# V's seven block products with 128 moving columns a matmul in place of 256, in a two-layer graph attention kernel

## The chip, the cores and the metric

The kernel runs on one core of one Trainium2 chip. The metric is the device time of one execution in microseconds (us). Three runs of the kernel before are given; the median is 2369.56 us.

## The reference

There are 128 graphs of 128 nodes with 512 features each (`x`: 128 x 128 x 512, fp32) and one 128 x 128 adjacency matrix for each graph. Two layers follow one another, each with a residual and a layer norm:

```python
def layer0(x, adj):                          # multi-head attention, 8 heads of 64
    q, k, v = x @ Wq + bq, x @ Wk + bk, x @ Wv + bv
    logits = einsum('bqhd,bkhd->bhqk', q, k) / sqrt(64)
    attn = softmax(where(adj > 0, logits, -1e9), axis=-1)
    return relu(einsum('bhqk,bkhd->bqhd', attn, v) @ Wo + bo)

def layer1(h, adj):                          # one-head graph attention
    Wh = h @ W
    e = leaky((Wh @ a1)[:, :, None] + (Wh @ a2)[:, None, :])
    att = softmax(where(adj > 0, e, -9e15), axis=1)
    return leaky(einsum('bij,bjf->bif', att, Wh))

x = layernorm(x + layer0(x, adj))
x = layernorm(x + layer1(x, adj))
```

The change touches only `x @ Wv`, the product that makes V.

## The kernel before

**Tiling.** Graphs are worked on in groups of four (`GROUP = 4`), that is 512 tokens; there are 32 groups. For each group, `products(g)` makes Q, K and V. Each of the three is a 512 x 512 by 512 x 512 product in fp32, done by Strassen's scheme on 256 x 256 blocks: seven block products in place of eight, with sums of blocks formed beforehand and results added afterwards. `group_product` holds it: `multiply` issues the TensorE work of one block product, `read` copies a partial sum out of PSUM on ScalarE (ACT), `add` adds a PSUM block to such a copy on VectorE (DVE) and writes a quarter of the result.

**One block product.** A block product contracts over 256 (two steps `kc` of 128) and gives 256 x 256 (two halves `m` of 128 rows). So `multiply` issues four calls of `nc.tensor.matmul`, each with a stationary block of 128 x 128 and a moving block of 128 x 256. In the profile every fp32 call appears as two pairs of records, LDWEIGHTS (engine PEld, the load of the stationary block) and MATMUL (engine PE), so a block product is 8 loads and 8 matmuls, and the seven of a group are 56 of each.

**Which operand is stationary.** For Q and K (`transposed_out=True`) the weight block is stationary and x moves, so the result has features on the partitions. For V (`transposed_out=False`) the block of x (128 tokens) is stationary and the weight block moves: 256 columns of features. V's weight blocks don't stay on chip. `wv` is in DRAM, and `fetch` brings one block product's weights at a time into a ring of three tiles:

```python
        def fetch():
            if todo:
                n = todo.pop(0)
                ring[n] = work.tile([P, 2, HALF], F32, name="wv_n", bufs=3)
                nc.sync.dma_start(ring[n], wv[n])
```

In the trace V's instructions are therefore those of line L367 that read `wv_n`; Q's and K's read `wq` and `wk` at the same line. The PSUM tiles are `st_y`, `st_w` and `st_x`, one bank each, 128 x (2 x 256) fp32.

**Other TensorE work.** `pair_product` (L448) does the same scheme for pairs of graphs with `wo` and `w1`, at 256 or 257 moving columns. `Softmax.scores` (L520, tile `lg`) multiplies 64-row operands with 128 moving columns, in the two row halves of the array alternately. `Softmax.attend` (L600, tile `p_oT`) uses 64-column stationary blocks with 128 moving columns, in the two column halves alternately. `Edge.product` (L841, tile `p_h`) has 512 moving columns. A few transposes (`p_x`, `p_e`, `p_busy`) load a 128 x 128 block and move 128 columns.

**Order.** The kernel writes the order of all instructions on every engine by hand (`manual_schedule` for TensorE, VectorE, ScalarE, SyncE and GpSimd). A loop over graphs calls `group()` and `pair()` between the steps of the softmax and the edge attention, so that block products stand between the pieces of other work; the last four graphs follow a written plan. [...]

Of the kernel before, what the change touches and what calls it, by code (L numbers as in the profile page):

```python
# [24 lines left out]
def kernel(  # L25
# [59 lines left out]
    nc = tc.nc  # L85
    B, P, D = x.shape
# [208 lines left out]
    def strassen(bank, multiply, read, add):  # L295

        p, t = {}, {}

        def product(role, n, start=False):
            def run():
                if start:
                    p[role] = bank(role)
                multiply(p[role], n, start)

            return run

        def copy(name, o):
            def run():  # L310
                t[name] = read(name, p["y"], o)

            return run

        def block(h, o, role, name=None):
            return lambda: add(h, o, p[role], t.get(name))

        return {
            "p1": product("y", 0, True),
            "t0": copy("t0", 0),  # L320
            "p5": product("w", 4, True),
            "p6": product("y", 5),
            "t2": copy("t2", 1),
            "p2": product("x", 1, True),
            "c11": block(0, 0, "x", "t0"),
            "p7": product("y", 6),
            "t3": copy("t3", 1),
            "c22": block(1, 1, "w", "t3"),
            "p4": product("y", 3),
            "c21": block(1, 0, "y"),  # L330
            "p3": product("w", 2),
            "c12": block(0, 1, "w", "t2"),
        }
# [7 lines left out]
    def copy_out(dst, p, o, bias):  # L341

        if bias is None:
            nc.scalar.copy(dst, p)  # L344
            return
        for m in range(2):
            col = bias[:, 2 * o + m : 2 * o + m + 1]
            nc.scalar.activation(dst[:, m, :], p[:, m, :], AF.Identity, bias=col)  # L348

    def group_product(g, turn, weight, out, transposed_out, bias=None):  # L350

        def bank(role):

            tag = "abc"[("ywx".index(role) - turn) % 3]
            return ps_st.tile([P, 2, 2 * P], F32, name=f"st_{role}", tag=tag)

        def multiply(p, n, start):
            w, xs = weight(n), XS[g][n]  # L360
            for m in range(2):
                cols = slice(m * P, (m + 1) * P)
                for kc in range(2):
                    lhs, rhs = xs[:, kc, cols], w[:, kc, :]
                    if transposed_out:
                        lhs, rhs = w[:, kc, cols], xs[:, kc, :]
                    nc.tensor.matmul(  # L367
                        p[:, m, :],
                        lhs,
                        rhs,  # L370
                        start=start and m == 0 and kc == 0,
                        stop=True,
                        skip_group_check=True,
                    )

        def read(name, p, o):
            t = work.tile([P, 2, 2 * P], F32, name=f"st_{name}")
            copy_out(t, p, o, bias)
            return t

        def add(h, o, p, t):
            if t is None:
                copy_out(out(h, o), p, o, bias)
            else:
                nc.vector.tensor_add(out(h, o), p, t)

        return strassen(bank, multiply, read, add)

    def products(g):
# [1033 lines left out]
```

## Time and profile before

| What | Value |
|---|---|
| Median of 3 runs | 2369.56 us (2368.99 to 2372.61) |
| Profiled execution | span 2364.5 us from its first to its last instruction |
| Device time less span | 5.1 us, with the median of the runs (the page gives no own time for the profiled execution beside its span) |
| TensorE clock granted, mean | 0.998 |
| PE busy, matmul records | 2330.4 us, 13362 records |
| PEld busy, weight-load records | 1976.3 us, 13362 records |
| DVE, ACT, POOL busy | 1836.7, 1507.4, 769.9 us |
| Mean DMA rate | 167 GB/s |
| V's matmul records (line L367 on `wv_n`) | 1792, which is 32 groups of 56 |

How to read it: a record of PE is one matmul and its duration contains a pipeline that overlaps the next record. So the duration of a record (379 ns for 256 columns) is not the step from one record to the next (some 216 ns). Where a stream of matmuls is at stake, the step between starts counts. A load (PEld) is recorded for each matmul and lies beside the matmul in front of it.

### The profile page before, as it was taken

The page shows a single profiled execution, that of the slowest core. Times are in us where ns is not written, and L with a number is a line of the kernel's source. Part 1 is how long each engine was busy: PE and PEld are TensorE (multiplying, and loading weights), DVE is VectorE, ACT ScalarE, POOL GpSimd, SP SyncE. Part 2 cuts the span into 40 slices and gives each one's busy share as a digit, 9 for nine tenths or more (in the row PEclk, how much of TensorE's full clock was granted, in tenths as well). Part 3 has the DMA queues.
Part 4 walks back from the last instruction along what each step waited for, and adds up shares of the span by engine and source line. Part 5 has one row for each costly group of instructions (what it writes and reads, how often), then busy time and mean ns, then how long its engine had stood idle before and what let it go on. Part 6 is the DMA issues. An engine that isn't in the chain of part 4 may idle for free.

```text
span 2364.5 us, 43985 instructions
## 1 busy us (share of the span) xinstructions
PE 2330.4 (99%) x13362; PEld 1976.3 (84%) x13362; DVE 1836.7 (78%) x3718; ACT 1507.4 (64%) x5459; POOL 769.9 (33%) x1191
## 2 busy tenths in 40 slices
PE   8999999999999999999999999999999999999997
PEld 7878888888888888888888888888888888888875
DVE  5677787877878877878778778778787787787778
ACT  3656666667666666666576666666665766666675
POOL 2232333323333323333233333233332333332325
PEclk9999999999999999999999999999999999999999
DMA  6655555555555555555555555555555555555453
GB/s 196 189 158 164 169 165 178 163 164 169 173 158 175 166 168 165 168 170 173 163 171 167 163 175 168 168 163 170 172 169 164 170 168 163 176 167 168 152 164 114
DMA packets 435564, 395.31 MB, mean 167 GB/s; under 512 B 108280, under 2 KB 339328, under 8 KB 435328
## 3 DMA queue, kind: packets, MB, share of 16 engines
q1 hardware_dynamic: 435008, 392.23, 54.2%
q8 instruction: 107, 1.75, 0.3%
q14 instruction: 129, 1.06, 0.2%
q10 hardware_dynamic: 320, 0.26, 0.0%
HBM read 248.58 MB, written 143.72 MB: 166 GB/s over the span
## 4 chain that ended last, share of the span: by engine, by line
PE 85%; DVE 5%; DMA 4%; ACT 3%; issue 1%; SPq 1%; POOL 1%; DVEq 0%; POOLq 0%; ACTq 0%
PE st_y L367 25%; PE p_y L448 16%; PE st_w L367 13%; PE p_w L448 8%; PE st_x L367 6%; PE lg L520 5%; PE p_oT L600 4%; PE p_h L841 4%; PE p_x L448 4%; ACT pa L568 1%; DMA paz<-pa_dram 1%; DMA pa_dram<-pa 1%; DVE st L644 1%; DVE pa L534 1%; DVE nmax L543 0%
## 5 line engine op out<-in xcount | busy, mean ns | idle before, releaser
L650 POOL TENSOR_SCALAR ve<-mv 128x1 f32<-128x1 f32 x256 | 69.8, 273 | 1425.4 <-DVE mv L646 1420.0
L554 ACT ACTIVATE pa<-pa,nmax 128x128 f32<-128x128 f32 x1008 | 393.4, 394 | 5.6 <-DVE nmax L543 5.5
L568 ACT ACTIVATE pa<-pa,rs 128x128 f32<-128x128 f32 x1008 | 326.6, 391 | 28.5 <-DVE rs L564 28.5
L344 ACT COPY st_t<-st_y 128x512 f32<-128x512 f32 x192 | 111.0, 578 | 158.9 <-PE st_y L367 83.2
L459 ACT COPY pr_t<-p_y 128x257 f32<-128x257 f32 (+1 forms) x375 | 137.3, 366 | 110.8 <-PE p_y L448 109.9
L348 ACT ACTIVATE st_t<-st_y,b_cols 128x256 f32<-128x256 f32 x192 | 79.9, 467 | 198.9 <-PE st_y L367 198.9
L554 ACT ACTIVATION_READ_ACCUMULATOR pa<-pa,nmax 128x1 f32 x1008 | 192.3, 191 | 0.0
L587 DVE STREAM_TRANSPOSE pa<-paz 128x1024 f32<-128x1024 f32 x126 | 156.9, 1245 | 18.1 <-DMA paz<-pa_dram 15.6
L534 DVE TENSOR_TENSOR pa<-lg,mf 128x512 f32<-128x512 f32 x252 | 161.0, 680 | 0.2 <-PE lg L520 0.2
L614 ACT ACTIVATE oT<-p_oT,b_cols 128x128 f32<-128x128 f32 x504 | 137.1, 381 | 33.8 <-PE p_oT L600 33.6
L543 DVE TENSOR_REDUCE nmax<-pa 128x8 f32<-128x1024 f32 x126 | 151.7, 1204 | 2.2
L652 POOL TENSOR_TENSOR rstd<-ve,mhalf 128x1 f32<-128x1 f32 x256 | 146.2, 571 | 21.3
L600 PEld LDWEIGHTS p_oT<-pa,v 128*64 128x64 f32 x2016 | 108.6, 137 | 49.5 <-issue 23.7
L520 PE MATMUL lg<-kT,qT 64*128 64x128 f32 x2048 | 132.1, 279 | 0.0
L448 PE MATMUL p_y<-wo,oT 128*128 128x256 f32 x504 | 129.6, 380 | 1.7 <-ACT p_y L469 1.7
L448 PE MATMUL p_y<-w,x1T 128*128 128x257 f32 x496 | 128.8, 382 | 1.7 <-ACT wk L459 1.6
L448 PE MATMUL p_y<-wo,oS 128*128 128x256 f32 x504 | 129.5, 379 | 0.5 <-ACT pr_t L459 0.5
L520 PEld LDWEIGHTS lg<-kT,qT 64*128 64x128 f32 x2048 | 119.4, 188 | 12.3 <-issue 11.6
L448 PE MATMUL p_y<-w,x1S 128*128 128x257 f32 x496 | 128.0, 380 | 0.2 <-ACT wk L459 0.2
L600 PE MATMUL p_oT<-pa,v 128*64 128x128 f32 x2016 | 125.0, 276 | 2.3 <-DVE pa L587 1.9
L367 PE MATMUL st_y<-wv_n,xT 128*128 128x256 f32 x512 | 121.3, 380 | 3.3 <-ACT st_t L344 3.3
L367 PE MATMUL st_y<-xT,wk 128*128 128x256 f32 x512 | 124.0, 385 | 0.0
(201 smaller groups left out, 5869.6 us busy)
## 6 DMA issues: line engine op xcount, KB each, us to landing
pa_dram<-pa SPq DMA_DIRECT2D x126, 512.0 KB, 2.9
paz<-pa_dram SPq DMA_DIRECT2D x504, 128.0 KB, 2.8
wv_n<-wv SPq DMA_DIRECT2D x224, 256.0 KB, 3.0
x<-in_x_dram SPq DMA_DIRECT2D x128, 256.0 KB, 2.9
x_dram<-x SPq DMA_DIRECT2D x128, 256.0 KB, 2.3
xz<-x_dram SPq DMA_DIRECT2D x512, 64.0 KB, 2.0
xz<-in_x_dram SPq DMA_DIRECT2D x496, 64.0 KB, 2.3
out_dram<-z SPq DMA_DIRECT2D x120, 256.0 KB, 2.5
```

The source lines that it names most:

```text
L367: nc.tensor.matmul(p[:, m, :], lhs, rhs, start=start and m == 0 and kc == 0, stop=True, skip_group_check=True,)
L448: nc.tensor.matmul(p[:, :width], xs()[n][:, kc, :], w[:, PLACE[n], kc, :], start=start and kc == 0, stop=True, skip_group_check=True,)
L459: nc.scalar.copy(t[:, :width], p[:, :width])
L520: nc.tensor.matmul(self.lg[r][:, c, :], q[rows, c, cols], k[rows, c, cols], start=c == 0, stop=True, skip_group_check=True,)
L534: nc.vector.tensor_add(by_head[:, r * NC : (r + 1) * NC], self.lg[r].rearrange("p c (b k) -> p c b k", b=4), mf.unsqueeze(1).to_broadcast( ...
L543: nc.vector.tensor_reduce(self.nmax, by_head, AX.XY, ALU.max, negate=True)
L554: nc.scalar.activation(self.pa[:, :, h, :], self.pa[:, :, h, :], AF.Exp, bias=self.nmax[:, h : h + 1], accum_out=self.sums[:, h : h + 1],)
L568: nc.scalar.activation(self.pa[:, :, h, :], self.pa[:, :, h, :], AF.Copy, scale=self.rs[:, h : h + 1])
L587: nc.vector.transpose(self.paT.rearrange("p h (a i) -> p a h i", i=32), self.paz.rearrange("p a (h k) -> p a h k", k=32),)
L600: nc.tensor.matmul(self.oT[r * HD : (r + 1) * HD, c, :], v[:, h * HD : (h + 1) * HD], self.paT[:, r * NC + c, :], start=c == 0, stop=True, ...
L614: nc.scalar.activation(OT[pair][:, c, h * P : (h + 1) * P], self.oT[:, c, :], AF.Identity, bias=b_cols[:, 1, c : c + 1],)
L652: nc.gpsimd.tensor_tensor(self.r, ve, mhalf, ALU.pow)
```

## The change

Where the output is not transposed, which holds for V alone, each call of 256 moving columns becomes two calls of 128 moving columns. The two calls use the same stationary block of x, and each call brings its own load of that block. The output columns, the order of the contraction steps and everything after the product stay. For Q and K `width` is 256 and the loop runs once. The `start` flag stays on the first call that writes into a fresh bank.

```diff
                     if transposed_out:
                         lhs, rhs = w[:, kc, cols], xs[:, kc, :]
-                    nc.tensor.matmul(
-                        p[:, m, :],
-                        lhs,
-                        rhs,
-                        start=start and m == 0 and kc == 0,
-                        stop=True,
-                        skip_group_check=True,
-                    )
+                    width = 2 * P if transposed_out else P
+                    for at in range(0, 2 * P, width):
+                        nc.tensor.matmul(
+                            p[:, m, at : at + width],
+                            lhs,
+                            rhs[:, at : at + width],
+                            start=start and m == 0 and kc == 0 and at == 0,
+                            stop=True,
+                            skip_group_check=True,
+                        )
```

A block product of V is then eight calls of 128 x 128 by 128 x 128 in the program's order, where it was four; the other engines' instructions and their order are those of before.

## The prediction

> **What bounds the kernel now.** I read the page's busy table first, then its slices, then the chain of work that ended last:
>
> ```profile
> span 2364.5 us, 43985 instructions
> PE 2330.4 (99%) x13362; PEld 1976.3 (84%) x13362; DVE 1836.7 (78%) x3718; ACT 1507.4 (64%) x5459; POOL 769.9 (33%) x1191
> PEclk9999999999999999999999999999999999999999
> PE 85%; DVE 5%; DMA 4%; ACT 3%; issue 1%; SPq 1%; POOL 1%; DVEq 0%; POOLq 0%; ACTq 0%
> ```
>
> PE is busy in every slice, at full granted clock, and 85% of the chain is PE. So TensorE's stream sets the time, and time added to that stream is added to the kernel unless it falls ahead of a stall that it fills. PE's busy time is made of records that overlap, so I don't count with it: I count steps from one matmul's start to the next. This is the timeline of PE early in the run, one row for a run of records (start, length, name, count):
>
> ```profile
> 10.37 1.04 PE L944 MATMUL p_x<-ident,x_turned 128*128 128x128 f32 x8
> 11.24 1.89 PE L367 MATMUL st_x<-xT,wq 128*128 128x256 f32 x8
> ...
> 20.83 1.89 PE L367 MATMUL st_y<-xT,wk 128*128 128x256 f32 x8
> 22.56 1.89 PE L367 MATMUL st_y<-xT,wq 128*128 128x256 f32 x8
> ```
>
> Eight records of 256 columns run from 20.83 to 22.56 us: 216 ns each. Eight transposes of 128 columns run from 10.37 to 11.24 us: 109 ns each. Taken from the individual starts in the trace, leaving stalls out: V's 256-column records step by 215.7 ns (1729 steps), transposes by 109.2 ns (17 steps).
>
> The next view is the groups by line with shapes kept apart (count, then busy us, mean ns, idle before):
>
> ```profile
> L520 PE MATMUL lg<-kT,qT 64*128 64x128 f32 x2048 | 132.1, 279 | 0.0
> L600 PE MATMUL p_oT<-pa,v 128*64 128x128 f32 x2016 | 125.0, 276 | 2.3 <-DVE pa L587 1.9 <-DVE rt L835 0.4
> L367 PE MATMUL st_y<-wv_n,xT 128*128 128x256 f32 x512 | 121.3, 380 | 3.3 <-ACT st_t L344 3.3
> L520 PEld LDWEIGHTS lg<-kT,qT 64*128 64x128 f32 x2048 | 119.4, 188 | 12.3 <-issue 11.6 <-DVE mf L498 0.3 <-DVE pa L534 0.3
> L600 PEld LDWEIGHTS p_oT<-pa,v 128*64 128x64 f32 x2016 | 108.6, 137 | 49.5 <-issue 23.7 <-PE st_y L367 22.0 <-DVE pa L587 2.6
> L367 PEld LDWEIGHTS st_y<-wv_n,xT 128*128 128x128 f32 x512 | 96.8, 190 | 18.0 <-ACT st_t L344 4.8
> ```
>
> A load's record depends on its columns: 137 ns for 64, 188 to 190 for 128, whether 64 or 128 rows take part. V's load (190 ns) today lies beside a matmul that takes 215.7 ns. The question is what such a load costs beside one of 109 ns.
>
> **What the Trainium skill says.** "TensorE: Matmul & The Clock Gate", section "LDWEIGHTS (loading the stationary operand)", puts a load at columns / 1.2 ns: 107 ns for 128, 53 for 64. The trace agrees in the slope (190 - 137 = 53 ns for 64 columns) and shows some 83 ns on top, which can be a latency that overlaps. The same page, "What happens when you issue a matmul", says that a load is pulled ahead of the matmul in flight into a background buffer; here each load starts 1 to 3 ns after the start of the matmul before it. Its "Back-to-back issue gap" gives N / 2.4 + 2.5 ns for a matmul alone, but 81 ns, not 56, for bf16 pairs of load and matmul at N = 128: that section warns of short moving blocks. "FP8 and Floating Point Precision", "TensorE Precision Notes", has true fp32 in four passes; each call here shows as two records, so two passes each: 2 x 256 / 2.4 + 2.5 = 215.8 ns against 215.7 measured, and 2 x 128 / 2.4 + 2.5 = 109.2 against 109.2.
>
> **The change, step by step.** Removed: 32 groups x 7 products x 8 = 1792 matmul records of 256 columns, with as many loads: 1792 x 215.7 ns = 386.5 us of TensorE's stream. Added: 3584 of 128 columns and 3584 loads of 128 x 128. Their step is the unknown.
>
> *Lower bound*, 109.2 ns: the array's own time, as in the transposes. Their loads have 141 ns records, so they don't test V's load. It gives 3584 x 109.2 - 386.5 = +4.9 us, which is one more fixed cost of some 2.5 ns for each old record.
>
> *The nearest rows.* L520 has loads of the full 128 columns (188 ns) beside 128 moving columns, and each row half of the array steps by 111.7 ns (1784 steps, 111 to 112); L600, with the short 137 ns loads, steps by 109.2. So a 188 ns load does not show its full record, only 107 ns and a handover of a few ns, and it is just longer than the matmul in front. L520 uses half the rows. The full array is seen where a transpose is followed by an ordinary matmul, whose 190 ns load must then hide behind 128 columns. A window of the groups view at such a place, ending within its first matmul:
>
> ```profile
> L944 PE MATMUL p_x<-ident,x_turned 128*128 128x128 f32 x3 | 0.5, 273 | 0.0
> L367 PE MATMUL st_x<-xT,wq 128*128 128x256 f32 x1 | 0.4, 382 | 0.0
> ```
>
> The matmul is recorded 109 ns after the transpose, but lasts 382 ns where its like last 379, and the next starts 219 ns on, not 216: it really began 3 ns late. Six of the transposes `p_e` near the end run into the next product without a stall: 108 to 110 ns, and where 257 or 256 columns follow (five), again 382 or 383 and 218 or 219. So 112 ns holds for the full array, once; sustained it is seen only in L520.
>
> *Value taken*: 111.7 ns. 3584 x 111.7 = 400.3 us, less 386.5: **+13.8 us**. By product: 16 x 111.7 - 8 x 215.7 = +61 ns on 1.73 us. *Upper bound*: if a full-array stream paid the 2.5 ns between 109.2 and 111.7 once more, 114.2 ns, +22.8 us.
>
> *The joints.* The record after a V product has its load behind 128 columns instead of 256, and the first record of a product still has a 256-column one in front of it; the count of short steps stays 3584. A semaphore that a next load waits for is needed no earlier than now: the last short matmul begins 109 ns later than the long one did. Before L520 and L600 the trace shows 309 ns after a 256-column record and 203 after a 128-column one: the same 94 ns, so nothing is lost there. The last record's tail shrinks from 379 to 272 ns but starts about 109 later: the readers on ACT and DVE get each product when its columns end, 61 ns later than now.
>
> *What hides some of it.* No wait, DMA or PSUM bank is added. The instruction stream grows by 3584 on PE; L520 runs two loads and two matmuls in 111.7 ns, twice V's density, so issue is not the limit: nothing. The weight fetches (`wv_n`, ring of three) have the same bytes, and start up to 61 ns later a product; covered by two ring tiles of lead. The `v` adds (DVE) and copies (ACT) wait for PE, and what stands behind them in order shifts with PE. A longer V fills stalls that other engines set. PE's waits:
>
> ```profile
> PE st_y L367 <- ACT st_t L344: 3.3, 3, 1.9
> PE st_y L367 <- DMA wv_n<-wv: 1.7, 1, 1.7
> PE st_w L367 <- DVE x1T L246: 0.5, 2, 0.3
> PE st_w L367 <- DMA wv_n<-wv: 0.3, 1, 0.3
> ```
>
> The ACT waits are in the first 200 us and follow from V's own copies. The rest, measured as starts later than the step allows, is three stalls behind DVE's x1T (832, 1050, 1267 us: 0.5, 0.4, 0.3) and four on `wv_n` (0.3 to 1.9 us, the largest at 2273): 4.4 us together. The fetches hang on PE's own release of the ring, so I credit little of those: 1.5 us absorbed in all (my choice; 0 to 4). **Sum: 13.8 - 1.5 = +12.3 us.** The sum stands against the profiled span, 2364.5 us, giving 2376.8; with the 5.1 us around it, which are the median less the span (the page has no time of its own for that execution), 2381.9, against the median of 2369.56: +0.52%.
>
> **The rivals.**
> *The load binds nowhere, so hardly anything shows* (not slower). The place is the handover from load to matmul: if the load of a full array in a stream is ready within the array's 109.2 ns, the bill is 4.9 us, less 1.5: +3.4 us, 2373.0. It decides below 109.5 ns, where the net falls under 4.7 us. Two runs differ by about 0.2% (4.7 us) before I would call them different. For: transposes and L600 step by 109.2. Against: their loads are short, and both places with full loads show 112. If the second load of the same block were left out, contrary to the change's words, this is the time as well. Below nothing I see no way: no column is saved and no wait is removed; the stalls it might move total 4.4 us.
> *Loads are not hidden in a stream.* The skill's 81 against 56 ns means 25 ns for each pair: 3584 x 25 + 4.9 = +94 us, about 2464. Wholly serial, 109 + 107 = 216 ns a record, would be +388 us. For: the section named, and that today's V never tests a load behind 109 ns. Against: L520 at 111.7, and the joints.
>
> **How the numbers follow.** The load just binds, 111 to 114.2 ns (2379 to 2392): 0.85, and this is the likeliest, 2381.9. Nothing binds: 0.09. Exposed loads, over 2400: 0.05. Something unforeseen that ends below -0.2%: 0.01. The range leaves out the exposed loads, and takes in the lower bound's case: 2373 to 2391. Chances: faster 0.01, within 0.2% 0.09, slower 0.90.
>
> **What would show it.** PE and PEld with 15154 records each. V's rows as 128x128, x3584, some 272 to 276 ns for a matmul and 188 to 192 for a load. A V product of 16 records in 1.79 us where eight took 1.73; Q's and K's still 1.73. Idle of PE unchanged within 3 us. Steps of 109 ns mean the first rival; steps over 120, or a V row with load idle in front, the second. I am also wrong if the steps are 112 but the time stays or grows otherwise: then stalls moved, and PE's waits must name them.

## The result, and the profile after

The changed kernel takes 2378.59 us (median of 4 runs, 2375.91 to 2381.42) against 2369.89 us for the kernel before (4 runs): +8.7 us, ratio 1.0041, 95% interval 1.0027 to 1.0054. The forecast was 2381.9 us, +12.3 us. A second measurement on another occasion gave 2375.32 us (18 runs) against 2367.28 us (28 runs): +8.0 us, ratio 1.0033, interval 1.0025 to 1.0042. So the kernel became slower by 0.3 to 0.4%.

The busy table, the granted clock and the chain of the page after, in the order in which those of before were shown:

```profile
span 2374.1 us, 47569 instructions
PE 2342.3 (99%) x15154; PEld 2040.3 (86%) x15154; DVE 1837.2 (77%) x3718; ACT 1511.9 (64%) x5459; POOL 770.5 (32%) x1191
PEclk9999999999999999999999999999999999999999
PE 89%; DVE 3%; DMA 3%; ACT 2%; issue 1%; SPq 1%; POOL 0%; DVEq 0%; POOLq 0%; ACTq 0%
```

The reader sees 1792 records more on PE and on PEld, and nothing more anywhere else; the span has grown by 9.6 us (2364.5 to 2374.1). PE's share of the chain went from 85% to 89%: the other engines lead the end less often. PE's busy time grew by 11.9 us. It has time that records share only once, but it also counts a record as busy while that record waits for its load, so the steps between starts are the measure.

The groups by line with shapes apart (records, then busy us, mean ns of one, idle before). The line numbers are 2 higher than before, and V's product is at L369:

```profile
L522 PE MATMUL lg<-kT,qT 64*128 64x128 f32 x2048 | 132.1, 279 | 0.0
L369 PE MATMUL st_y<-wv_n,xT 128*128 128x128 f32 x1024 | 125.0, 275 | 2.4 <-ACT st_t L344 2.4
L369 PEld LDWEIGHTS st_y<-wv_n,xT 128*128 128x128 f32 x1024 | 124.0, 192 | 6.7 <-ACT st_t L344 3.4
L522 PEld LDWEIGHTS lg<-kT,qT 64*128 64x128 f32 x2048 | 119.4, 188 | 11.9 <-issue 11.3 <-DVE spare L536 0.3
```

V's matmuls are recorded with 275 ns (the median too), where the transposes, with loads of 141 ns, have a median of 273; V's loads are recorded with 192 ns, and had 190 before. The 2 ns more are a late start like the 3 ns that the prediction read from the joints. PE's timeline in a stretch of V:

```profile
1022.63 1.03 PE L450 MATMUL p_x<-wo,oT 128*128 128x256 f32 x4
1023.50 1.95 PE L369 MATMUL st_y<-wv_n,xT 128*128 128x128 f32 x16
1025.28 1.03 PE L450 MATMUL p_y<-wo,oS 128*128 128x256 f32 x4
```

Sixteen records run from 1023.50 to 1025.28 us, 1.78 us, where eight took 1.73. From the individual starts, stalls left out, V steps by 111.52 ns (3525 steps). Q and K still step by 215.8.

The time from start to start, summed over all records of a kind, says where the 9.6 us are. A stall here is the part of a step that goes beyond the free step of its kind:

| Records | Before, us | After, us | Difference |
|---|---|---|---|
| V, steps without stalls | 1792 x 215.74 ns = 386.6 | 3584 x 111.52 ns = 399.7 | +13.1 |
| V, time over that step | 10.9 | 9.8 | -1.1 |
| Q and K | 784.7 | 783.5 | -1.2 |
| `pair_product` | 789.6 | 788.9 | -0.6 |
| all other, with the start and the end of the span | 392.7 | 392.2 | -0.5 |

The stream of V got 13.1 us longer, and stalls on PE got some 3.5 us shorter.

### The profile page after: what moved, and what is told of

Same layout as the page of the kernel before. It is cut to its first block, busy times and chain, and to the rows that moved or that the text cites. A ratio compares the mean times of both kernels' runs of the same rounds, so it can differ in the third digit from the quotient of the medians.

```text
span 2374.1 us, 47569 instructions
## 1 busy us (share of the span) xinstructions
PE 2342.3 (99%) x15154; PEld 2040.3 (86%) x15154; DVE 1837.2 (77%) x3718; ACT 1511.9 (64%) x5459; POOL 770.5 (32%) x1191
## 4 chain that ended last, share of the span: by engine, by line
PE 89%; DVE 3%; DMA 3%; ACT 2%; issue 1%; SPq 1%; POOL 0%; DVEq 0%; POOLq 0%; ACTq 0%
PE st_y L369 26%; PE p_y L450 17%; PE st_w L369 13%; PE p_w L450 8%; PE st_x L369 6%; PE lg L522 5%; PE p_oT L602 5%; PE p_x L450 4%; PE p_h L843 4%; DMA paz<-pa_dram 1%; ACT pa L570 1%; DMA pa_dram<-pa 1%; DMA wv_n<-wv 0%; SPq L583 0%; DVE st L646 0%
## 5 line engine op out<-in xcount | busy, mean ns | idle before, releaser
L654 POOL TENSOR_TENSOR rstd<-ve,mhalf 128x1 f32<-128x1 f32 x256 | 146.5, 572 | 21.3
L369 PEld LDWEIGHTS st_y<-wv_n,xT 128*128 128x128 f32 x1024 | 124.0, 192 | 6.7 <-ACT st_t L344 3.4
L522 PEld LDWEIGHTS lg<-kT,qT 64*128 64x128 f32 x2048 | 119.4, 188 | 11.9 <-issue 11.3
L369 PEld LDWEIGHTS st_y<-wv_n,xS 128*128 128x128 f32 x1024 | 123.4, 192 | 6.7 <-issue 2.0
L369 PE MATMUL st_y<-wv_n,xT 128*128 128x128 f32 x1024 | 125.0, 275 | 2.4 <-ACT st_t L344 2.4
```

The source lines that it names most:

```text
L369: nc.tensor.matmul(p[:, m, at : at + width], lhs, rhs[:, at : at + width], start=start and m == 0 and kc == 0 and at == 0, stop=True, skip ...
L522: nc.tensor.matmul(self.lg[r][:, c, :], q[rows, c, cols], k[rows, c, cols], start=c == 0, stop=True, skip_group_check=True,)
L654: nc.gpsimd.tensor_tensor(self.r, ve, mhalf, ALU.pow)
```

## The experiments

Three questions were left. Is the load really the longer side of the 111.5 ns, or is it a fixed cost of each short matmul? Does it belong to V's blocks? And how much of a longer stream do PE's stalls swallow: a fixed amount or a share? The edits below are against the changed kernel.

**V halved once more, for the time alone** (no edit).

> The changed kernel once more, beside runs of the kernel before on the same chip. Both theories: V's records step by 111.5 ns, the stream of V grows by 3584 x 111.5 - 1792 x 215.7 = +13.1 us. Theory A (the time that V's longer stream fills is a fixed handful of stalls): +9 us over before, as in the first four runs (2378.59 against 2369.89). Theory B (the first runs were slow or quick by chance): anything from +5 to +13 us.

Measured: 2375.32 us, +8.0, as above. Profiled span 2372.1 us; V's step 111.52 ns. The stall total differs by 2 us between the two profiled executions of the same kernel, so what is filled isn't an exact number. The size of the first result holds.

**Q and K halved, V whole.**

```diff
-                    width = 2 * P if transposed_out else P
+                    width = P if transposed_out else 2 * P
```

> Q and K in halves of 128 columns, V whole: 3584 old records become 7168. The stationary block is a weight, not x. If the load's handover sets the step whatever is loaded: 111.5 ns, stream +3584 x (2 x 111.5 - 215.8) = +25.8 us. Theory A (a fixed 4 us of stalls is filled): +22 us, about 2392. Theory B (a third of any lengthening is filled): +17 us, about 2387. Rival C (the 111.5 ns belongs to V's x blocks alone, Q's and K's step by 109.2): +9.3 us of stream, about 2375 to 2379.

Measured: 2388.59 us against 2367.28, ratio 1.0086 (1.0069 to 1.0103), +21.3 us. Q's and K's step is 111.51 ns (7122 steps), so the stream grew by 25.9 us. Rival C falls: the step is that of a weight block too. Some 4.6 us were filled, about as much as when V's stream grew by 13.1, which is what theory A says.

**Q, K and V halved.**

```diff
-                    width = 2 * P if transposed_out else P
+                    width = P
```

> All of Q, K and V in halves of 128: 5376 old records become 10752, stream +38.8 us at 111.5 ns. Theory A (fixed 4 us filled): +35 us, about 2405. Theory B (a third filled): +26 us, about 2396. The step is 111.5 ns in all three.

Measured: 2398.86 us, ratio 1.0125 (1.0107 to 1.0143), +31.6 us for a stream that grew by 39.0. This lies between the two theories: 7.4 us filled, neither a fixed 4 nor a third.

**The loops over column halves and contraction steps exchanged.** In the changed kernel the two calls on one block of x follow each other; here another block comes between them.

```diff
-                for kc in range(2):
...
-                    for at in range(0, 2 * P, width):
+                for at in range(0, 2 * P, width):
+                    for kc in range(2):
```

> V in halves of 128, but the loop over column halves lies outside the loop over contraction steps: the same matmuls and loads, and no two calls in a row use the same block of x. Main theory (each load is paid as it comes, 111.5 ns a record): as the changed kernel, within 0.2%, steps 111.5 ns, load records 192 ns. Rival (loading the same block again is cheaper than another, or writing the same half of the bank again costs): steps of 113 to 116 ns, +3 to +16 us over the changed kernel, or below 111 ns and quicker.

Measured: 2376.26 us, ratio 1.0032 (1.0021 to 1.0043), beside 1.0033 for the changed kernel on the same chip. Step 111.51 ns, loads 192 ns. So it makes no difference whether the next call brings the same block of x or another one, nor whether it writes the same half of the bank. Each call has two load records, and no run shows whether these two carry the same part of the fp32 block; so a load that repeats the one just before it, value for value, may not occur in either order.

**V in quarters of 64 moving columns.** The matmul becomes much shorter than the load.

```diff
-                    width = 2 * P if transposed_out else P
+                    width = 2 * P if transposed_out else P // 2
```

> V in quarters of 64 moving columns: 7168 records, each with a load of the whole 128 x 128 block. Main theory (the load and its handover take some 111.5 ns whatever the matmul's length, and are the longer side): step 111.5 ns, stream 7168 x 111.5 - 386.6 = +413 us, about 2779. Rival (the load is hidden, 111.5 is the array's time plus a fixed 4.8 ns for each record): step 53.3 + 4.8 = 58 ns, stream +30 us, about 2396.

Measured: 2770.32 us against 2368.29, ratio 1.1710 (1.1683 to 1.1737), +402.0 us. This is the timeline of PE, two rows:

```profile
1022.78 3.68 PE L369 MATMUL st_y<-wv_n,xT 128*128 128x64 f32 x32
1026.30 1.08 PE L450 MATMUL p_y<-wo,oS 128*128 128x256 f32 x4
```

Thirty-two records take 3.52 us, 110 ns each. The first recorded step of a product is 55 ns, and the mean of the others is 111.66. Half the columns don't shorten the step at all. The groups view has the loads at the same 192 ns:

```profile
L369 PEld LDWEIGHTS st_y<-wv_n,xT 128*128 128x128 f32 x2048 | 238.3, 192 | 5.2 <-ACT st_t L344 2.0
L369 PE MATMUL st_y<-wv_n,xT 128*128 128x64 f32 x2048 | 235.8, 273 | 1.4 <-ACT st_t L344 1.4
```

The 111.5 ns are the load's period, and the rival's 58 ns are out of question. A matmul's record contains the wait for its own load. The first record of a product, whose load lay beside a 256-column matmul, lasts 218 ns (median of 185); the others last 275 (median), some 56 ns more. The loads say the same: in free stretches each starts 1 to 3 ns after the recorded start of the matmul in front, here 56 ns after it. So the columns begin that much after the recorded start, and the first recorded step is short.

**V in parts of 160 and 96 moving columns.** As many matmuls and loads as in the changed kernel, only their sizes differ.

```diff
-                    width = 2 * P if transposed_out else P
-                    for at in range(0, 2 * P, width):
+                    for at, end in [(0, 2 * P)] if transposed_out else [(0, 160), (160, 256)]:
...
```

The call then writes and reads the columns `at:end`.

> V in two unequal parts of 160 and 96 moving columns: as many matmuls and loads as the changed kernel, 3584. Main theory (each step is the longer of array and load): 160 columns step by 133.3 + 2.5 = 135.8 ns, 96 columns by 111.5, together 247.3 against 223.0 in the changed kernel and 215.7 before: +56.6 us of stream on before, about 2423. Rival (array plus a fixed cost for each record): 138 + 85 = 223, +13 us, as the changed kernel, about 2379.

Measured: 2413.38 us, ratio 1.0192 (1.0177 to 1.0207), +45.1 us. PE's timeline, in which one row holds the records of both sizes:

```profile
1039.78 2.11 PE L368 MATMUL st_y<-wv_n,xT 128*128 128x160 f32 x16
1041.73 1.06 PE L449 MATMUL p_y<-wo,oS 128*128 128x256 f32 x4
```

Sixteen records take 1.95 us, where the changed kernel's take 1.78. In a product free of stalls the pattern of two 160s and two 96s repeats every 495 ns (starts 1040.242, 1040.737, 1041.232 us), so a 160 and a 96 take 247.5 ns together, against the 247.3 worked out from the longer side of each and 223 for an array with a fixed cost. The single recorded starts step by 165, 136, 82 and 112 ns, but again the records contain their waits: the second 96 and the first 160, whose loads lie beside a 96, last 275 and 328 ns, and the other two 246 and 299. With these 29 ns taken as wait, the matmuls begin 136, 136, 112 and 112 ns apart. The stream grew by 1792 x (247.5 - 215.7) = 57 us; the time grew by 45, so 12 us were filled. The main theory's 2423 is missed by 10 us, because it credited nothing for stalls.

**V with stationary blocks of 64 columns.** The loads become short, the moving side keeps its 128 columns.

```diff
+                        for half in [slice(P)] if transposed_out else [slice(HD), slice(HD, P)]:
                             nc.tensor.matmul(
-                            p[:, m, at : at + width],
-                            lhs,
+                                p[half, m, at : at + width],
+                                lhs[:, half],
...
```

The other lines of the call are moved in by one step and stay as they are.

> V with 128 moving columns, and each stationary block cut into two of 64 columns that go to the two column halves of the array in turn, as L600 does: 7168 records, whose loads are short (137 ns records instead of 192). Main theory (the load of 128 columns is what makes 111.5 ns of 109.2): each column half steps by 109.2 ns, 3584 x 109.2 - 386.6 = +4.8 us of stream; in addition each change between whole-array and half-array work costs some 94 ns, as before L600 and after L520 in the kernel before, twice for most of the 224 products: up to +42 us. Together about +43 us, 2411. Rival (111.5 ns belongs to 128 columns written to V's bank, or to V's order of calls, whatever is loaded): steps of 111.5 ns, 8 us more than the main theory.

Measured: each column half steps by 109.2 ns (6412 steps), with 137 ns loads. With the short load the 2.3 ns are gone, in the same bank and with the same data. The time is 2419.80 us (2 runs) against 2364.52, +55.3 us, more than the 43 expected. The timeline shows why:

```profile
1041.14 1.03 PE L451 MATMUL p_x<-wo,oT 128*128 128x256 f32 x4
1042.10 1.97 PE L370 MATMUL st_y<-wv_n,xT 128*64 128x128 f32 x32
1044.00 1.13 PE L451 MATMUL p_y<-wo,oS 128*128 128x256 f32 x4
1044.97 1.24 PE L370 MATMUL st_w<-xT,wk 128*128 128x256 f32 x5
```

The four records of `p_x` take 0.96 us to the next start instead of 0.86, and the four of `p_y` behind the product take 0.97. Besides the 94 ns ahead of the first record, the first step inside is longer as well: 160 instead of 109 ns on the way in, 320 instead of 216 on the way out. So a change costs some 144 ns in and 198 out. There are 184 ways in, 152 from whole-array work and 32 from the scores, where the trace shows the same 94 ns and 160. There are 182 ways out to whole-array work, less the 32 that followed the scores before. That is 26 + 30 = 56 us, and 61 with the 4.8 of the stream, of which some 6 to 8 were filled: the time grew by 55.3 us and the profiled span by 53.3. The expectation had counted only the first 94 ns of each change.

**What is filled, and where.** Each start of a block of scores stands at the same place of the program in all runs. So the time of a run at such a place, less that of the kernel before, can be set against the stream added up to there. The table shows the difference, the microseconds filled so far:

| Run (stream added in all) | to 200 us | to 1431 us | to 2009 us | to the end |
|---|---|---|---|---|
| changed kernel (13.1) | 0.7 | 5.1 | 4.0 | 3.4 |
| again (13.1) | 0.5 | 4.5 | 4.2 | 5.5 |
| other order (13.1) | 1.5 | 4.2 | 3.2 | 4.0 |
| Q and K (25.9) | 2.2 | 4.7 | 4.6 | 3.4 |
| Q, K and V (39.0) | 3.2 | 6.1 | 5.5 | 6.2 |
| 160 and 96 (57) | 3.4 | 8.3 | 8.6 | 10.6 |
| 64 (414) | 6.4 | 11.4 | 12.1 | 14.6 |

The table is from one profiled execution of each run, and that of the 64 was the quickest of its four. By the medians of all runs, 4 to 5 us are filled at the end where the stream grew by 13.1 or 25.9, 7.4 where it grew by 39.0, and 12 both at 57 and at 414. A stream that grew thirty times as much fills about three times as much: it is a stock of stalls, not a share. Most of it lies in the first 1431 us. One stall can be watched. This is PE in the kernel before:

```profile
1045.97 1.03 PE L448 MATMUL p_y<-w,x1T 128*128 128x257 f32 x4
1047.00 1.11 PE L448 MATMUL p_w<-w,x1T 128*128 128x257 f32 x4
1047.95 1.89 PE L367 MATMUL st_y<-wv_n,xT 128*128 128x256 f32 x8
1050.05 1.97 PE L367 MATMUL st_w<-wv_n,xT 128*128 128x256 f32 x8 [0.21 <-DVE x1T L246]
```

and this is the same place in the changed kernel:

```profile
1047.88 1.03 PE L450 MATMUL p_y<-w,x1T 128*128 128x257 f32 x4
1048.76 1.03 PE L450 MATMUL p_w<-w,x1T 128*128 128x257 f32 x4
1049.62 1.95 PE L369 MATMUL st_y<-wv_n,xT 128*128 128x128 f32 x16
1051.47 2.02 PE L369 MATMUL st_w<-wv_n,xT 128*128 128x128 f32 x16
```

Before, the steps between rows are 1.03, 0.95 and 2.10 us, where the free ones are 0.87, 0.87 and 1.73. After, they are 0.88, 0.86 and 1.85, where 1.78 is free. PE comes to `st_y` 1.67 us later, while DVE's transposes `x1T`, which `st_w` waits for by the trace, end only 1.46 us later (at 1051.46 in place of 1050.00 us). With the shorter waits in the rows ahead, some 0.5 us of waiting is gone. In the trace the lead of the kernel before, which grows by 0.42 us for each group in calm stretches, shrinks here by 0.24 us between 1033 and 1106 us.

## Why the prediction was right, point by point

**TensorE's stream sets the time.** Right. PE's share of the chain rose, and in all variants the time followed the stream within the stock of stalls, once the changes to half-array work are counted with it.

**The load is just longer than a matmul of 128 columns.** Right, and now shown from three sides: 64 columns leave the step at 111.66 ns, 160 and 96 add up as the longer of array and load, and short loads give 109.2. The prediction had it for the full array only in single steps, at joints, and sustained only for half the rows in L520; that this would carry over was not shown then, and it did. The size was taken as 111.7 ns and is 111.52: 13.1 us where 13.8 was reckoned, 61 ns a product foreseen and some 58 found.

**The joints, the instruction stream, the fetches.** Right as far as the sum tells: the 3584 steps at one size account for V's stream, and nothing new stands in front of it.

**What hides some of it.** This is the term that was mis-sized: 1.5 us foreseen, 3.4 to 5.5 found in three executions with the same stream, at and beyond the end of the 0 to 4 that was given. The step that failed is the list of stalls. It counted those in front of V's own records. There the time over the step fell by 1.1 us, near the 1.5, but that was in part luck: the waits on DVE's `x1T` went as it had hoped, those on `wv_n` grew from 2.0 to 2.6 us, and 0.9 us came from a wait on ACT in the first 200 us that it had set aside as following from V's own copies (1.9 us before, 1.0 after). The other 2.3 us came from records that it had not counted: Q and K 1.2, `pair_product` 0.6, all other 0.5. A V product that ends later also lets the engines catch up ahead of other work: the start-up gave 0.5 to 1.5 us, and stalls of 0.6 us at `p_oT` (380 us), 0.3 at `p_w` (829 us) and 0.45 at `p_y` (214 us) are not there in the changed kernel. The caution over the `wv_n` fetches was half right. This is from PE's list of waits after:

```profile
PE st_y L369 <- ACT st_t L344: 2.4, 3, 1.0
PE st_y L369 <- DMA wv_n<-wv: 2.0, 2, 1.7
...
PE st_w L369 <- POOL xS L276: 1.2, 1, 1.2
...
PE st_w L369 <- DMA wv_n<-wv: 0.6, 1, 0.6
```

The DVE x1T entry has gone from PE, the largest wait on a fetch is still 1.7 us, and the other fetch stalls went from places like 398 and 615 us to others, such as 1996 and 2070.

**The sum against the median.** The prediction put 5.1 us around the span, by taking the median for the profiled execution. That reading was wrong. An execution of the changed kernel with a span of 2374.1 us took 2375.91 us, 1.8 us around, and in all executions on record for which both are known, those of the kernel before among them, it is 1.7 to 1.9 us. So the profiled execution of before took some 2366.3 us (an estimate, 2364.5 + 1.8) and was a quick one; the rest of the 5.1 us is the spread of the runs. It makes no difference to the +12.3, which is a difference of streams.

**The rivals.** "The load binds nowhere" would have been 109.2 ns, and "loads are not hidden" 134 or 216; both are excluded by 111.52. What a full load adds to a record of 128 columns is 2.3 ns here, not the 25 with which the second rival was priced. The measured 8.0 to 8.7 us lie between the first rival's 3.4 and the 12.3 because of the fill, not because of the step.

What stays open: how far the step would fall with a short load beside fewer than 128 columns, which no run tried (at 128 columns, short loads leave the array as the longer side, at 109.2 ns). And which of the stalls will be filled in a given execution. Two executions of the same program differed by 2 us in this, and new stalls of up to 0.8 us appeared at other places; no run separated their causes. That the vanished stalls vanished because other engines caught up is read from traces like the one above, and no experiment took a single stall away.

## What to carry to other kernels

A load of the stationary block was free here only as long as the matmul in front of it was longer, so compare its period, not its recorded length, with the step. By an estimate from the free steps (109.2 ns at 128 columns and 215.7 at 256, so 0.83 ns a column) the array reaches the load's 111.5 ns at about 131 moving columns in fp32; at 128 the split cost 3.4% of the split stream. The records just behind a few short matmuls, 3 ns longer than their like, told this ahead of any run. This kernel, with one engine busy at 99%, still had a stock of small stalls, and part of what lengthened that engine's stream went into it: price the stream from its steps, and give the stalls anywhere behind the lengthened work as the margin, not only those in front of it.

## What the runs showed of the hardware

- A load of 128 x 128 fp32, recorded with 190 to 192 ns, has a period of 111.5 to 111.7 ns in a stream, at 64 as at 128 moving columns.
- A call on the same block as the call before steps as one on another block does (111.52 and 111.51 ns).
- The recorded length of a matmul contains the wait for its load: 275 ns at 64 and at 128 moving columns when the load sets the step, but 218 and 273 ns when it doesn't.
- A change from whole-array to half-array work (column halves) cost some 144 ns and the way back 198, in two parts each: before the first record and in the step behind it.
